# The first image's chain: one activation table load, weights quantized later, the ring cleared by GpSimd, two PSUM banks for one convolution

## The chip, the cores and the metric

The kernel runs on one core of one Trainium2 chip. The metric is the device time of a whole run in microseconds (us); smaller is better. A core has five engines with a queue of instructions each: PE (TensorE, matmuls, with PEld for its weight loads), DVE (VectorE), ACT (ScalarE), POOL (GpSimd) and SP (SyncE, which only issues DMAs here). Each engine runs its own instructions in order and waits at semaphores for the others. Sixteen DMA engines serve the core.

## The reference

The input x is 32 images of 256 channels by 32 x 32 pixels. Two layers follow each other, each with a residual:

```
x = x + conv_quant(groupnorm(x))      # 3x3, 256 -> 256 channels
x = x + involution(groupnorm(x))      # 7x7 filters made from the pixels themselves
```

`groupnorm` has 32 groups of 8 channels, without scale and shift: subtract the group's mean, divide by the root of its variance plus 1e-5. `conv_quant` rounds its input and its weights to fp16 (clipped at 65504), multiplies with fp32 accumulation, rounds and clips the result to fp16 and adds a bias. The involution makes, per pixel, 16 filters of 49 taps by two 1x1 convolutions with a fixed normalization and a ReLU between them, and applies each filter to the 16 channels of its group:

```
y   = relu(bn(w1 @ xn))                        # 64 channels
w   = w2 @ y + b2                              # 16 groups x 49 taps per pixel
out[g, c, h, w] = sum over taps of w[g, tap, h, w] * xn[g, c, neighbour(tap)]
```

## The kernel before

An image is held as a tile of 128 partitions by 2 halves of channels (`CH`) by 1024 pixels (`N`). Images go through a software pipeline that `tc.manual_schedule()` writes out by hand: the loop at L537 counts a step `n`, and in each step it asks which piece of which image is due. The order in which instructions are issued in that loop is the order in which each engine's queue holds them. An image takes `per` = 2M = 16 steps, and starts `-FRONT` = 56 steps ahead of its own sums, so that the work of about four images stands in flight.

The generator `front(b)` (L275) yields step by step the first part of image `b`'s work. In its order:

- group norm of layer 0. `add_up` (L207) sums x on ACT, one instruction per half, with the sum going into a column of `sums_sb`. `group` (L214) turns these into sums by group on DVE: transpose (L220, `across`), reduce (L222, `total`), transpose back (L226, `back`). `means` (L229) puts the mean on ACT, `squares` adds up the squares on ACT (L210 again), `variances` calls `group` again and takes the square root on ACT (L241, `s`), then `scales` and `finish` make `rstd` and `off` by eight small instructions, and `apply` writes the normalized image as fp16 into `xq` (L269, ACT).
- the convolution of layer 0. An image has four units (`units`, two halves of the pixels by two halves of the output channels). A unit is 18 matmuls from `xq` and `wq` (L320, PE) into one PSUM bank, `pc`. Then DVE clips it to fp16 (L334, `q`), adds bias and x (L336, `x`), and ACT adds up the new x for the next group norm (L210). `pc` comes from the pool `ps_c`, which has one buffer: the next unit waits for the `q` of the last.
- group norm of layer 1, then the product with `w1` (L368, `py`) and the transposes of the pixels (L383, `pt`); `py` and `pt` share one bank of the pool `ps_m` (tag "m").

After `front`, `weights` (L390) multiplies by `w2` and DVE adds `b2` while it writes the filters into a ring in SBUF, `w_sb` (L416); `scatter` (L454) sends them by DMA into the DRAM buffer `wd`, issued by SP (L465); `load_bands` (L467) reads them back as diagonals of a band matrix, issued by POOL and one in eight by SP (L478); `sums` (L489) multiplies bands and pixels on PE (L503), and `add_windows` adds them to x (L519).

Ahead of the loop stands the set-up (L122 to L194). It loads the first image, clears tiles on GpSimd, clears the ring `w_sb` on DVE (L147), loads the fp32 weights of the convolution into the first two of the three band tiles, which aren't in use yet (L154), clips and rounds them to `wq` on DVE (L155), clears the two band tiles on GpSimd (L156), and loads the small constants.

The tiles of the pool `const` lie one behind the other in SBUF in the order in which they are made, and the other pools behind them.

Of the kernel before, what the change touches and what calls it, by code (L numbers as in the profile page):

```python
# [9 lines left out]
F32 = mybir.dt.float32  # L10
AF = mybir.ActivationFunctionType
ALU = mybir.AluOpType

P = 128
B, C, H, W = 32, 256, 32, 32
N = H * W
NT = 512
RT = NT // W
CH = C // P
# [10 lines left out]
F16_MAX = 65504.0  # L30
# [35 lines left out]
FRONT = -56  # L66
# [5 lines left out]
def tile_quant_conv_then_involution(  # L72
# [16 lines left out]
    nc = tc.nc  # L89
    PSUM = bass.MemoryType.PSUM  # L90

    const = ctx.enter_context(tc.tile_pool(name="const", bufs=1))
# [7 lines left out]
    ps_m = ctx.enter_context(tc.tile_pool(name="ps_m", bufs=1, space=PSUM))  # L100
# [26 lines left out]
    xq = const.tile([P, CH, H, W], F16, name="xq")  # L127
    eps = const.tile([P, 1], F32, name="eps")
    nc.gpsimd.memset(eps, GN_EPS)
    three_halves = const.tile([P, 1], F32, name="three_halves")  # L130
    nc.gpsimd.memset(three_halves, 1.5)

# [5 lines left out]
    bands = [const.tile([P, SIDES, WINC * WB + XR], F32, name=f"band_{i}") for i in range(NBAND)]  # L138
# [5 lines left out]


    w_sb = const.tile([P, 2, RING, G, WIN], F32, name="w_sb")
    nc.vector.memset(w_sb, 0.0)  # L147
    wd = dram.tile([H, S, WPIX], F32, name="wd")
    acc = [ps_acc.tile([P, RG, NT], F32, name=f"acc_{d}") for d in range(SIDES)]

    wq = const.tile([P, CH, K0 * K0, C], F16, name="wq")
    for kh in range(CH):
        wf = bands[kh].rearrange("p d n -> p (d n)")[:, : K0 * K0 * C].rearrange("p (k c) -> p k c", c=C)
        nc.sync.dma_start(wf, w0[kh * P : (kh + 1) * P])  # L154
        nc.vector.tensor_scalar(wq[:, kh], wf, F16_MAX, -F16_MAX, ALU.min, ALU.max)  # L155
        nc.gpsimd.memset(bands[kh], 0.0)  # L156
    w2_sb = const.tile([P, K1, SW], F32, name="w2_sb")
    for i in range(2):
        nc.sync.dma_start(w2_sb[i * CR : (i + 1) * CR], w2)
# [24 lines left out]
    for col, cols, at, n in (  # L184
        (0, S, K1 * WB, XR),
        (PAD1, PAD1, 0, PAD1 * WB),
        (W, PAD1, (K1 - PAD1) * WB, PAD1 * WB),
    ):
        to = bass.AP(
            tensor=wd.tensor,  # L190
            offset=wd.offset + col * WPIX + at,
            ap=[[ROW, H], [WPIX, cols], [1, n]],
        )
        nc.sync.dma_start(to, bands[NBAND - 1][:H, 0, :n].unsqueeze(1).to_broadcast([H, cols, n]))  # L194

    class GroupNorm:

# [77 lines left out]
    def front(b):  # L275
# [30 lines left out]
        for s in range(4 * len(units) + 2):  # L306
            u, i = divmod(s, 4)
            if u < len(units):
                nt, mh = units[u]
                if i == 0:  # L310
                    pc = ps_c.tile([P, NT], F32, tag="pc", name="pc")
                for n in range(sum(CONV[:i]), sum(CONV[: i + 1])):


                    k = n if n < K0 * K0 else CH * K0 * K0 - 1 - n
                    kh, k = n // (K0 * K0), (k + K0 * K0 // 2) % (K0 * K0)
                    di, dj = k // K0 - PAD0, k % K0 - PAD0
                    r0, r1 = max(nt * RT, -di), min((nt + 1) * RT, H - di)
                    c0, c1 = max(0, -dj), min(W, W - dj)
                    nc.tensor.matmul(  # L320
                        pc.rearrange("p (r c) -> p r c", c=W)[:, r0 - nt * RT : r1 - nt * RT, c0:c1],
                        wq[:, kh, k, mh * P : (mh + 1) * P],
                        xq[:, kh, r0 + di : r1 + di, c0 + dj : c1 + dj],
                        start=n == 0,
                        stop=n == CH * K0 * K0 - 1,
                    )

            u, i = divmod(s - 3, 4)
            if 0 <= u < len(units) and i < 3:
                nt, mh = units[u]  # L330
                cols = slice(nt * NT, (nt + 1) * NT)
                if i == 0:
                    q = work.tile([P, NT], F16, tag="q", name="q", bufs=1)
                    nc.vector.tensor_scalar(q, pc, F16_MAX, -F16_MAX, ALU.min, ALU.max)  # L334
                elif i == 1:
                    nc.vector.scalar_tensor_tensor(  # L336
                        xt[:, mh, cols], q, bias_sb[:, mh : mh + 1], xt[:, mh, cols], ALU.add, ALU.add
                    )
                else:
                    gn.add_up(xt, nt, mh, nt * NT, (nt + 1) * NT, AF.Identity)  # L340
            yield
# [112 lines left out]
    def scatter(b, k):  # L454

        at = (b * H + k * TR) % RING
        for dj in range(K1):
            t, e = divmod(dj, 2)
            to = bass.AP(
                tensor=wd.tensor,  # L460
                offset=wd.offset + k * TR * ROW + dj * WPIX + (K1 - 1 - dj) * WB,
                ap=[[WPIX, TW], [ROW, TR], [1, WB]],
            )
            rows = w_sb[t * TW : (t + 1) * TW, e, at : at + TR]
            nc.sync.dma_start(to, rows.rearrange("p s g r -> p s (g r)"))  # L465
# [23 lines left out]
    def sums(b, m):  # L489

        k, d = divmod(m, SIDES)
        j0 = 0 if d else PAD1
        band = bands[(b * K + k) % NBAND][:, d]
        px = pixels[(b * K + k) % NPIX][:, d]
        for h in range(CH):
            for v in range(2):
                for g, at, top, f, l in windows(b, m):
                    p = slice(g * KP, (g + 1) * KP)
                    of = band[p, g * XR + j0 * WB : g * XR + (j0 + WINI) * WB]
                    of = of.rearrange("p (j g r) -> p j g r", g=G, r=WIN)  # L500
                    for t in range(T):
                        a = h * T + t
                        nc.tensor.matmul(  # L503
                            at[t * TW : (t + 1) * TW, h, :, f - top : l - top],
                            px[p, a, v * GC : v * GC + TW],
                            of[:, :, 2 * a + v, f - top : l - top],
                            start=(h, v) == (0, 0),
                            stop=(h, v) == (CH - 1, 1),
                        )

    def add_windows(b, m):

        d = m % SIDES
        to = x_tiles[b].rearrange("p h (r c) -> p h r c", c=W)
        j0 = d * (JC - PAD1)
        for g, at, top, f, l in windows(b, m):
            x_at = to[:, :, f:l, j0 : j0 + WINI]
            of = at.rearrange("p h j r -> p h r j")[:, :, f - top : l - top]
            nc.vector.tensor_tensor(x_at, of, x_at, ALU.add)  # L519

    def store(b, k):

        cols = slice(k * NT, (k + 1) * NT)
        nc.sync.dma_start(out[b].rearrange("(h p) n -> p h n", p=P)[:, :, cols], x_tiles[b][:, :, cols])
# [5 lines left out]
    def due(n, lag):  # L530

        b, i = divmod(n - lag, per)
        return (b, i) if 0 <= b < B else (None, None)

    with tc.manual_schedule():
        fronts = {}
        for n in range(FRONT, B * per + 2):  # L537
            b, i = due(n, FRONT)
            if i == 0:
                fronts[b] = front(b)  # L540
            later = list(fronts)
            for part in range(2):
                for b in list(later):
                    got = next(fronts[b], fronts)
                    if got is fronts:
                        fronts.pop(b)
                    if got is not LATER:
                        later.remove(b)
            b, i = due(n, 0)
            if b is not None and i % 2 == 0:  # L550
                sums(b, i // 2)
            b, i = due(n, 1)
            if b is not None and i % 2 == 0:
                add_windows(b, i // 2)
                if i // 2 == M - 1:
                    store(b, 1)
                    x_tiles.pop(b)

            b, i = due(n, 2)
            if b is not None and i == 2 * (M - 1 - SIDES):  # L560
                store(b, 0)
            b, i = due(n, -LEAD)
            if b is not None and i % 2 == 0:
                weights(b, i // 2 * WR)

            b, i = due(n, -LEAD + 1)
            if b is not None and i % 2 == 0:
                for k in range(K):
                    if i // 2 == min((k + 1) * TR // WR, H // WR - 1):
                        scatter(b, k)  # L570
            b, i = due(n, LOAD)
            if i == 0 and b > 0:
                x_tiles[b] = load_x(b)

            b, i = due(n, 3 - 4 * NBAND)
            if b is not None and i % 4 == 0:
                load_bands(b, i // 4)
# [37 lines left out]
```

## Time and profile before

| | us |
|---|---|
| median of 3 runs | 1411.43 (1402.78, 1411.43, 1411.64) |
| the profiled execution's own time | 1416.45 |
| its span, first to last instruction | 1414.7 |

| engine | busy us | share of the span | instructions |
|---|---|---|---|
| PE | 1265.2 | 89% | 29440 |
| DVE | 933.0 | 66% | 3180 |
| ACT | 729.8 | 52% | 1699 |
| POOL | 1003.5 | 71% | 1817 |

The row of the page that shows the DMA engines' busy share in 40 slices of the span, 35.4 us each, begins with 6, 0 and 9: busy while the first inputs are loaded, then idle, then busy at nine tenths to the end. By queue, q1 (issued by SP) carried 235.72 MB in 279904 packets and took 57.2% of the 16 engines' time; q0 (issued by POOL) carried 129.14 MB and took 34.5%.

A line of the timeline has the start and the duration in us, the engine, the line of the kernel, the operation, the output and input with their shapes, and the number of merged instructions. In brackets stands the idle time of the engine just before it, and what ended that idle time.

### The profile page before, as it was taken

To read this page: it belongs to the slowest core of one execution; us is meant where nothing else is said; L and a number is where in the kernel's file an instruction comes from. 1 tells how busy PE (TensorE), PEld (TensorE's weight loads), DVE (VectorE), ACT (ScalarE), POOL (GpSimd) and SP (SyncE) were. 2 spreads that over 40 slices of the span, in tenths; PEclk is the share of its full clock that TensorE was granted. 3 is DMA by queue.
4 is the path that set the end of the run, shared out by engine and by line. 5 is a ranking of instruction groups with operands and counts; after the bars stand their busy time and mean duration, and the time that the engine had idled before them with its cause. 6 is when DMAs were issued, how large, how long until landed. Compare 5 with 4: busy or idle time off the path is not lost.

```text
span 1414.7 us, 70076 instructions
## 1 busy us (share of the span) xinstructions
PE 1265.2 (89%) x29440; PEld 802.2 (57%) x29440; DVE 933.0 (66%) x3180; ACT 729.8 (52%) x1699; POOL 1003.5 (71%) x1817
## 2 busy tenths in 40 slices
PE   4899899999999899989999999999999999999665
PEld 1456565566565566655566556565566556655543
DVE  4567667767677677766767667767667676766642
ACT  5775555455555445555545555554556454553300
POOL 7067767686776777767777777677776767777774
PEclk9999999999999999999999999999999999999976
DMA  6099899999999999999999999999999999999995
GB/s 212 6 228 283 251 277 276 281 262 285 277 273 264 287 268 269 294 260 270 289 267 287 268 277 253 273 280 273 274 289 271 268 279 282 278 270 262 258 258 165
DMA packets 366232, 369.33 MB, mean 261 GB/s; under 512 B 78624, under 2 KB 308192, under 8 KB 365664
## 3 DMA queue, kind: packets, MB, share of 16 engines
q1 hardware_dynamic: 279904, 235.72, 57.2%
q0 software_dynamic: 86016, 129.14, 34.5%
q8 instruction: 234, 3.83, 1.2%
q14 instruction: 78, 0.64, 0.1%
HBM read 183.81 MB, written 180.74 MB: 258 GB/s over the span
## 4 chain that ended last, share of the span: by engine, by line
PE 47%; DMA 31%; issue 7%; POOL 5%; DVE 4%; ACT 3%; SPq 2%; POOLq 0%; DVEq 0%; ACTq 0%
DMA band<-wd 24%; PE pc L320 19%; PE acc L503 15%; PE pw L398 9%; DMA wd<-w_sb 7%; POOL band L478 5%; PE py L368 3%; DVE w_sb L416 2%; PE pt L383 2%; SPq L465 2%; ACT junk L210 1%; DVE x L519 0%; DVE w_sb L147 0%; ACT xn L269 0%; DVE q L334 0%
## 5 line engine op out<-in xcount | busy, mean ns | idle before, releaser
L478 POOL DMA_DIRECT2D band<-wd x1792 | 978.0, 548 | 397.8 <-DMA band<-wd 249.0
L416 DVE TENSOR_TENSOR w_sb<-pw,b_sb 128x16 f32<-128x16 f32 (+9 forms) x1920 | 454.0, 350 | 386.9 <-PE pw L398 363.2
L320 PE MATMUL pc<-xq,wq 128*128 128x496 f16 (+3 forms) x2304 | 536.5, 379 | 31.3 <-ACT xq L269 21.4
L503 PE MATMUL acc<-band,pixels 64*32 64x190 f32 (+1 forms) x16384 | 420.5, 323 | 78.9 <-DMA band<-wd 39.6
L503 PEld LDWEIGHTS acc<-band,pixels 64*32 64x32 f32 x16384 | 298.3, 108 | 171.1 <-issue 101.5
L320 PEld LDWEIGHTS <-wq 128*128 128x128 f16 x2304 | 206.4, 98 | 328.9 <-issue 114.6
L398 PE MATMUL pw<-w_sb,y 64*32 64x224 f32 (+1 forms) x8192 | 296.6, 333 | 31.1 <-issue 29.4
L519 DVE TENSOR_TENSOR x<-acc,x 128x380 f32<-128x380 f32 (+1 forms) x512 | 261.7, 511 | 35.7 <-PE acc L503 26.8
L398 PEld LDWEIGHTS pw<-w_sb,y 64*32 64x32 f32 x8192 | 182.8, 107 | 63.0 <-issue 43.9
L387 ACT COPY pixels<-pt 128x512 f32<-128x512 f32 x128 | 73.6, 575 | 238.2 <-PE pt L383 238.2
L210 ACT ACTIVATE junk<-x 128x512 f16<-128x512 f32 (+1 forms) x192 | 146.5, 763 | 20.7 <-DVE x L336 15.2
L210 ACT ACTIVATE junk<-x,mean 128x1024 f16<-128x1024 f32 x128 | 147.1, 1149 | 4.3
L241 ACT ACTIVATE s<-back,eps 128x2 f32<-128x2 f32 x64 | 18.9, 296 | 193.7 <-DVE back L226 193.6
L334 DVE TENSOR_SCALAR q<-pc 128x512 f16<-128x512 f32 x128 | 87.2, 682 | 16.5 <-PE pc L320 16.3
L269 ACT ACTIVATE xn<-x,off,rstd 128x512 f32<-128x512 f32 x128 | 96.1, 799 | 0.0
L336 DVE SCALAR_TENSOR_TENSOR x<-q,bias_sb,x 128x512 f32<-128x512 f16 x128 | 92.1, 719 | 0.2
L383 PEld LDWEIGHTS pt<-ident,xn 128*128 128x128 f32 x512 | 64.0, 142 | 27.4 <-issue 3.2
L383 PE MATMUL pt<-ident,xn 128*128 128x128 f32 x512 | 78.1, 275 | 0.9 <-ACT pixels L387 0.9
L231 ACT ACTIVATE mean<-back 128x2 f32<-128x2 f32 x64 | 12.7, 199 | 127.6 <-DVE back L226 127.6
L269 ACT ACTIVATE xq<-x,off,rstd 128x1024 f16<-128x1024 f32 x64 | 75.8, 1227 | 0.1
L368 PEld LDWEIGHTS py<-xn,w_sb 128*64 128x64 f32 x2048 | 63.0, 139 | 16.5 <-issue 8.1
L368 PE MATMUL py<-xn,w_sb 128*64 128x64 f32 x2048 | 67.8, 224 | 2.3 <-ACT xn L269 1.8
(40 smaller groups left out, 370.7 us busy)
## 6 DMA issues: line engine op xcount, KB each, us to landing
wd<-w_sb SPq DMA_DIRECT2D x896, 160.0 KB
band<-wd POOLq DMA_DIRECT2D x1792, 70.2 KB
x<-in_x SPq DMA_DIRECT2D x64, 512.0 KB
out<-x SPq DMA_DIRECT2D x64, 512.0 KB
band<-wd SPq DMA_DIRECT2D x256, 70.2 KB
band<-in_w SPq DMA_DIRECT2D x2, 1152.0 KB
w_sb<-in_w SPq DMA_DIRECT2D x2, 196.0 KB
wd<-band SPq DMA_DIRECT2D x2, 180.0 KB
```

What stands on the lines that cost most here:

```text
L210: nc.scalar.activation(junk[:, n0:n1], src[:, h, n0:n1], func, bias=bias, accum_out=self.sums[:, i : i + 1])
L269: nc.scalar.activation(dst, src, AF.Identity, bias=self.off[:, one], scale=self.rstd[:, one])
L320: nc.tensor.matmul(pc.rearrange("p (r c) -> p r c", c=W)[:, r0 - nt * RT : r1 - nt * RT, c0:c1], wq[:, kh, k, mh * P : (mh + 1) * P], xq[: ...
L334: nc.vector.tensor_scalar(q, pc, F16_MAX, -F16_MAX, ALU.min, ALU.max)
L336: nc.vector.scalar_tensor_tensor(xt[:, mh, cols], q, bias_sb[:, mh : mh + 1], xt[:, mh, cols], ALU.add, ALU.add)
L368: nc.tensor.matmul(py[i * CR : (i + 1) * CR, cols], w1_sb[:, kh, :], px[:, r : r + 2], start=kh == 0, stop=kh == CH - 1,)
L383: nc.tensor.transpose(pt[:, i, h * P : (h + 1) * P], xn[:, h, (m + i) * P : (m + i + 1) * P], ident)
L398: nc.tensor.matmul(pws[i][t * TW : (t + 1) * TW, r, : dj.stop - dj.start], y_sb[b % 2][half, (r0 // 2 + r) * W : (r0 // 2 + r + 1) * W], w ...
L416: nc.vector.tensor_tensor(to, pws[i][:p, r : r + rows, e, d0 * G : d1 * G].rearrange("p r (d g) -> p r d g", g=G), b2_sb[:p, e, d0 * G : d ...
L478: queue.dma_start(band[j::JC, :, j * WB : j * WB + WPIX], src)
L503: nc.tensor.matmul(at[t * TW : (t + 1) * TW, h, :, f - top : l - top], px[p, a, v * GC : v * GC + TW], of[:, :, 2 * a + v, f - top : l - top],
L519: nc.vector.tensor_tensor(x_at, of, x_at, ALU.add)
```

## The change

Four edits, all in the set-up or for the first image alone:

- Right behind `eps`, a one-column activation with the square root is issued on ACT, into a new tile `warm` of 128 x 1.
- The ring `w_sb` is no longer cleared on DVE in the set-up.
- The weights are only loaded in the set-up. Rounding them to `wq` and clearing the two band tiles goes into a function `quantize_weights`, which the loop calls in its third step (`n == FRONT + CH`), after the parts of `front` due in that step; the same function then clears `w_sb`, on GpSimd.
- The first image's units 1 and 3 take their PSUM bank from `ps_m` instead of `ps_c`.

```diff
     nc.gpsimd.memset(eps, GN_EPS)
+
+    warm = const.tile([P, 1], F32, name="warm")
+    nc.scalar.activation(warm, eps, AF.Sqrt)
     three_halves = const.tile([P, 1], F32, name="three_halves")
...
     w_sb = const.tile([P, 2, RING, G, WIN], F32, name="w_sb")
-    nc.vector.memset(w_sb, 0.0)
...
+    staged = []
     for kh in range(CH):
         wf = bands[kh].rearrange("p d n -> p (d n)")[:, : K0 * K0 * C].rearrange("p (k c) -> p k c", c=C)
         nc.sync.dma_start(wf, w0[kh * P : (kh + 1) * P])
-        nc.vector.tensor_scalar(wq[:, kh], wf, F16_MAX, -F16_MAX, ALU.min, ALU.max)
-        nc.gpsimd.memset(bands[kh], 0.0)
+        staged.append(wf)
...
+    def quantize_weights():
+
+        for kh in range(CH):
+            nc.vector.tensor_scalar(wq[:, kh], staged[kh], F16_MAX, -F16_MAX, ALU.min, ALU.max)
+            nc.gpsimd.memset(bands[kh], 0.0)
+        nc.gpsimd.memset(w_sb, 0.0)
...
                 nt, mh = units[u]
-                if i == 0:
+                if i == 0 and b == 0 and u % 2:
+
+                    pc = ps_m.tile([P, NT], F32, tag="m", name="pc")
+                elif i == 0:
                     pc = ps_c.tile([P, NT], F32, tag="pc", name="pc")
...
+            if n == FRONT + CH:
+                quantize_weights()
             b, i = due(n, 0)
```

In the built program, DVE's queue then begins with the three instructions of the first `group`, the two quantizations, and the next `group`; ACT's begins with the one table load and the activation into `warm`; the second table load is gone; PE, POOL and SP hold the same instructions in the same order as before, but for the memset of `w_sb` behind those of the two band tiles on POOL.

## The prediction

> **What bounds the kernel now.** I read the stage table first, because the change touches only the work of the first image and of the set-up. The columns are the stretch, its length, busy us (and instructions) of PE, PEld, DVE, ACT and POOL, then clock, DMA share and GB/s.
>
> ```profile
> 0.00:69.00 69.00, 43.11 (x325) 20.13 (x326) 32.16 (x73) 45.76 (x103) 25.46 (x25) 1.00 0.34 110
> 93.00:1350.00 1257.00, 1162.70 (x27817) 744.16 (x27818) 860.39 (x2962) 664.83 (x1550) 924.47 (x1694) 0.99 0.97 273
> ```
>
> From 93 us on the DMA engines are 97% busy and PE 92%: the long part is limited by both, and no edit speeds up either there. Before 69 us the DMA share is 0.34, nearly all of it loads. The first scatter of filters into the buffer wd is issued at 69.03 us; nothing of the long part can start without it. So the first 69 us are a prologue, and a microsecond off its chain is one off the end, unless a resource bound to absolute time takes its place. The timeline of the prologue shows that chain (start, duration, engine, line, operation; in brackets the idle time before it and who ended it):
>
> ```profile
> 4.68 1.28 ACT L210 ACT_TABLE_LOAD   x1 [4.68 <-DMA x<-in_x]
> 2.41 6.46 DVE L147 MEMSET w_sb<- 128x7680 f32 x1 [2.41 <-issue]
> 8.79 0.15 DVE L220 STREAM_TRANSPOSE across<-sums 128x32 f32<-128x32 f32 x1
> 9.08 1.88 DVE L155 TENSOR_SCALAR wq<-band 128x2304 f16<-128x2304 f32 x1
> 10.88 0.19 DVE L226 STREAM_TRANSPOSE back<-total 128x32 f32<-128x32 f32 x1
> 12.00 1.53 DVE L155 TENSOR_SCALAR wq<-band 128x2304 f16<-128x2304 f32 x1 [0.93 <-DMA band<-in_w]
> 13.93 1.28 ACT L241 ACT_TABLE_LOAD   x1
> 14.02 0.21 DVE L220 STREAM_TRANSPOSE across<-sums 128x32 f32<-128x32 f32 x1 [0.49 <-ACT junk L210]
> 15.22 0.29 ACT L241 ACTIVATE s<-back,eps 128x2 f32<-128x2 f32 x1
> 26.28 3.97 PE L320 MATMUL pc<-xq,wq 128*128 128x512 f16 x18 [0.78 <-DVE q L334]
> 36.44 0.21 DVE L220 STREAM_TRANSPOSE across<-sums 128x32 f32<-128x32 f32 x1
> 41.53 3.97 PE L320 MATMUL pc<-xq,wq 128*128 128x512 f16 x18 [1.77 <-ACT xq L269]
> ```
>
> The reader is to see four delays: a table load after x has landed; a memset and a quantization on DVE that hold the first mean; a second table load that ends at 15.21, just ahead of s; and 0.78 us in which PE waits for DVE to empty the one bank. Against these stands one line that the change cannot move: the second half of the weights lands at 12.00.
>
> [...]L140's took 5.97 us beside the DVE memset, L156's 5.97 each without one. [...]the first 18 matmuls took 6.36 us, the next 3.97.
>
> **The change part by part**, as times of the changed kernel.
>
> *Table load.* Two loads become one. The new one waits for no DMA, so it ends before x lands at 4.68; the warm activation needs eps, set at 0.98. The first sum starts at 4.7 instead of 5.98, the second when the other half of x is there (not later than 7.16; I take 5.9), and both end at 7.1, at worst 8.3.
>
> *DVE memset and order.* The memset moves to GpSimd, the quantizations behind the first mean's three instructions. The group step takes 0.7 us (from 14.02 to 14.7 in its second use), so the mean is at 7.8 instead of 11.10, and the squares end at 10.6 (2.5 us plus 0.3 for the mean). That alone would be 3.3 us. But in the new order of DVE both quantizations now stand ahead of the variance's transpose. The second waits for its DMA until 12.00 and takes 1.53: the transpose starts at 13.55 instead of 14.02, a gain of 0.47. The other 2.9 us are lost to this wait, and with them the worry over when x lands: up to 2.9 us later costs nothing. With 1.88 us, the first quantization's time, the gain would be 0.1.
>
> *Second table load gone.* s then follows at 13.55 + 0.7 = 14.25 instead of 15.22: **0.97 us** in all (0.6 to 1.0). PE starts at 18.17 instead of 19.14.[...]
>
> *Two banks.* Unit 0 ends at 24.54, and units 1, 2, 3 follow without the three waits of 0.78: at 24.55, 28.52, 32.49, ending at 36.46 (before: 39.76). Units 2 and 3 need q of units 0 and 1, done at 25.3 and 29.2. But PE is not what comes next: the second image's convolution waits for its xq on ACT (1.77 us in the last line above). That chain goes over DVE, where image 1's variance transpose stands behind x of unit 2. x of unit 2 comes 0.97 + 2 x 0.78 = 2.53 us earlier, at 33.2; the squares end at about 33.6, so the transpose stays bound by DVE and starts at 33.9 instead of 36.44. xq starts 3.8 us after it as before, at 37.7, and PE at 39.0 instead of 41.53. xq has one buffer and must wait for unit 3 to have read it, 36.46: slack 1.2 us. So **2.53 us** in all; the third 0.78 goes into PE's idle time. What is late next is ACT's chain.
>
> *GpSimd.* Its order gets one memset more, behind the two of the bands (to 26.0, as they still start at 14.14 behind the pixels' memsets). At L156's rate, 5.97 us for 7048 elements, 7680 take 6.5: done at 32.5. The first instruction that waits for it writes the ring at 60.81 - 2.5 = 58.3, and GpSimd's next own work, the band loads, stood at 77.32: cover of 26 and 42 us. No DMA issue moves past another on SP's or POOL's queue. What is new is that x of units 0 and 1[...] run beside a GpSimd memset. If they doubled to 1.5 us, unit 0's has 0.7 us of slack before unit 1's x, and unit 1's has about 0.35 before the squares bind: at most 0.4 us lost, below nothing excluded. I take 0.
>
> *One small tile more.* warm takes 32 bytes, and in the built program every tile behind it moves up by 32 (w_sb from 129312 to 129344). Taken as 0; see the last rival.
>
> Sum: -2.53 us.[...] Against the profiled execution's own 1416.45 us (span 1414.7 and 1.75 around it) that is 1413.9. The median shown is 5.0 us lower, at 1411.43; the forecast is set against it: **1408.9 us**. The three runs lie 9 us apart, more than three times the gain.
>
> **The rivals.**
>
> *Only the start counts.* If the second image's chain on ACT is held by something else (for example its x landing later than it now needs it), the banks bring nothing: -0.97, 1410.5. For it: image 1's x was issued at only 21.65. Against it: its first sum started at 27.91 with no wait for a DMA, and ACT wants it at about 26.9.
>
> *The gain is absorbed.* From 93 us on, PE and DMA take turns at the end of waits, and an earlier start may be spent in a different interleaving: 1411.4. Against it: between 40 and 70 us the DMA queues carry almost nothing (a share of 0.01), so the limiting stream itself starts earlier.
>
> *Slower: the shifted addresses.* [...]The 896 scatters of 160 KB are 229,376 rows. [...]queue 1 spent 57.2% of 16 x 1414.7 us on 279,904 packets, 46 ns each[...].
>
> **How the numbers follow.** Within 1% (14 us, about what can be told from no change) lies nearly everything above. The forecast's case gets 0.72, with a range of its own from 1401 to 1413 by the spread of the runs; only the start 0.06, absorbed 0.10, addresses 0.08 (of which 0.03 above 1%), unseen causes 0.04 on either side. Range: the runs' spread of 1402.8 to 1411.6 less 2.5 below[...]: **1400 to 1416**. Chances: faster 0.04, same 0.91, slower 0.05.
>
> **What would show it.** One table load, done before 4.7; the first mean near 7.8; the variance's transpose right behind a quantization that starts at 12.00; s near 14.25; no gap between the first image's four units; image 1's convolution near 39.0; the first scatter near 66.5. If that scatter comes 2.5 us early and the end doesn't, the gain was absorbed; if queue 1's share rises above 58%, the addresses cost. The forecast is wrong if the weights land at another time than 12.00, or if the long part's length between first scatter and end differs by more than the gain.

## The result and the profile after

Over 20 runs each, the median is 1405.6 us (1396.03 to 1412.58) against 1410.24 (1393.54 to 1419.45) before. The ratio of the runs is 0.9973, with a 95% interval of 0.995 to 0.9996: faster by 3.8 us, between 0.6 and 7.1. (The two medians lie 4.6 us apart.) The profiled execution took 1399.26 us, with a span of 1397.5.

The timeline of the changed kernel, with the lines that answer to those of before:

```profile
0.74 1.28 ACT L132 ACT_TABLE_LOAD   x1 [0.74 <-PEq L618]
...
6.99 0.21 DVE L229 STREAM_TRANSPOSE across<-sums 128x32 f32<-128x32 f32 x1 [6.99 <-ACT junk L219]
...
7.71 0.20 ACT L240 ACTIVATE mean<-back 128x2 f32<-128x2 f32 x1 [0.82 <-DVE back L235]
...
8.51 1.76 DVE L201 TENSOR_SCALAR wq<-band 128x2304 f16<-128x2304 f32 x1 [0.84 <-DMA band<-in_w]
...
12.08 1.44 DVE L201 TENSOR_SCALAR wq<-band 128x2304 f16<-128x2304 f32 x1 [1.81 <-DMA band<-in_w]
...
13.44 0.19 DVE L229 STREAM_TRANSPOSE across<-sums 128x32 f32<-128x32 f32 x1
...
14.14 0.30 ACT L250 ACTIVATE s<-back,eps 128x2 f32<-128x2 f32 x1 [3.62 <-DVE back L235]
...
18.06 18.05 PE L332 MATMUL pc<-xq,wq 128*128 128x512 f16 x72 [18.06 <-ACT xq L278]
...
38.81 3.97 PE L332 MATMUL pc<-xq,wq 128*128 128x512 f16 x18 [2.71 <-ACT xq L278]
...
66.34 11.95 SPq L477 DMA_DIRECT2D wd<-w_sb  x14
```

The mean is 3.4 us earlier than before (7.71 for 11.10), but s only 1.08 (14.14 for 15.22): in between, ACT is idle for 3.62 us, waiting behind the second quantization, which waits for its weights until 12.08 and ends at 13.52. The four units of the first image are now one row of 72 matmuls without a gap. Image 1's convolution starts at 38.81, after 2.71 us in which PE is idle. The first scatter is issued at 66.34 instead of 69.03; its line before was

```profile
69.03 12.12 SPq L465 DMA_DIRECT2D wd<-w_sb  x14
```

The stage table shows the long part as busy as before (length, busy us of PE, PEld, DVE, ACT and POOL, clock, DMA share, GB/s):

```profile
91.00:1333.00 1242.00, 1157.73 (x27700) 740.74 (x27683) 858.57 (x2960) 663.34 (x1548) 920.82 (x1688) 0.99 0.98 276
```

The two spans differ by 17.2 us, and only 2.69 of these lie ahead of the first scatter. The other 14.5 lie in the long part, which the change doesn't touch: 1331.2 us from first scatter to end here, 1345.7 before. The same length was between 1316 and 1346 us in the 14 profiles of this study. It shows no pattern by kernel, but one by chip: the four shortest come from the chip on which the kernel before is some 8 us faster too. So a single execution says nothing on a change of this size. The time of the first scatter says more, though it also moves between executions of one kernel, as a second profile of the change will show; the medians of many runs tell within some 3 us.

### The profile page after: what moved, and what is told of

It is laid out like the page before. It is cut to its first block, busy times and chain, and to the rows that moved or that the text cites. A ratio compares the mean times of both kernels' runs of the same rounds, so it can differ in the third digit from the quotient of the medians.

```text
span 1397.5 us, 70073 instructions
## 1 busy us (share of the span) xinstructions
PE 1263.0 (90%) x29440; PEld 801.1 (57%) x29440; DVE 926.6 (66%) x3179; ACT 727.9 (52%) x1699; POOL 1009.8 (72%) x1818
## 4 chain that ended last, share of the span: by engine, by line
PE 49%; DMA 30%; issue 6%; POOL 5%; DVE 4%; SPq 3%; ACT 2%; POOLq 0%; DVEq 0%; ACTq 0%
DMA band<-wd 23%; PE pc L332 20%; PE acc L515 15%; PE pw L410 9%; DMA wd<-w_sb 6%; POOL band L490 5%; PE py L380 3%; SPq L477 3%; DVE w_sb L428 2%; PE pt L395 2%; ACT junk L219 1%; DVE x L531 1%; DMA band<-in_w 1%; DMA x<-in_x 0%; ACT xn L278 0%
## 5 line engine op out<-in xcount | busy, mean ns | idle before, releaser
L332 PE MATMUL pc<-xq,wq 128*128 128x496 f16 (+3 forms) x2304 | 535.1, 378 | 28.1 <-ACT xq L278 21.3
```

The source lines that it names most:

```text
L332: nc.tensor.matmul(pc.rearrange("p (r c) -> p r c", c=W)[:, r0 - nt * RT : r1 - nt * RT, c0:c1], wq[:, kh, k, mh * P : (mh + 1) * P], xq[: ...
```

## The experiments

Each kernel is compared with runs of the kernel before on the same chip, in the order in which they stand here. Those medians were 1410.6 us for the first four kernels, 1411.5 for the next three, 1402.3 for the next four and 1410.8 for the last. The first scatter is read from one profile each. Six of the kernels were run once (the banks alone, the order alone, order and banks, the change once more, the memsets behind at first, the second bank for unit 1); of these only the profile is used, but for one time that is taken up at the end.

**The banks alone.**

```diff
# on the kernel before
-                if i == 0:
+                if i == 0 and b == 0 and u % 2:
+                    pc = ps_m.tile([P, NT], F32, tag="m", name="pc")
+                elif i == 0:
```

> The kernel before with the two-bank edit alone. Theory of the prediction (the banks take two of the three waits of 0.78 us off the second image's chain, through the variance's transpose that stands on DVE behind x of unit 2): xq for the first image as before (about 17.9 us), no gap between the first image's four units, image 1's convolution at about 40.0 instead of 41.5, and the first scatter at 67.4 to 67.5 instead of 69.0 (1.56 us earlier). Rival, that ACT's chain is held by something else, such as the second image's load: the gaps go, but the first scatter stays at 68.8 to 69.1.

Measured: xq at 17.87 as before, no gaps, and these two rows on PE:

```profile
19.15 16.79 PE L323 MATMUL pc<-xq,wq 128*128 128x512 f16 x72 [19.15 <-ACT xq L269]
38.65 5.66 PE L323 MATMUL pc<-xq,wq 128*128 128x512 f16 x18 [2.71 <-ACT xq L269]
```

Image 1's convolution starts at 38.65, 2.88 us earlier than before. About 1.9 of this are the two waits: from one q to the next there are 3.81 us instead of 4.75. The other 1.0 comes from a shorter cold phase, by which is meant the slow start of the first image's matmuls (before, its first 18 took 6.36 us and each later 18 took 3.97): the first q already stands at 24.54 instead of 25.54 although PE started as before. But its first 18 matmuls then took 5.66 us instead of 3.97, after PE had been idle for 2.71. The first scatter stands at 67.81 rather than 67.4: the mechanism holds for image 1's convolution, and a cost of 1.7 us shows that neither theory had.

**The order alone.** Both quantizations behind the first mean; two table loads, the ring's memset on DVE and one bank as before.

```diff
# on the kernel before
-        nc.vector.tensor_scalar(wq[:, kh], wf, F16_MAX, -F16_MAX, ALU.min, ALU.max)
-        nc.gpsimd.memset(bands[kh], 0.0)
+        staged.append(wf)
...
+            if n == FRONT + CH:
+                quantize_weights()      # without the memset of w_sb
```

> The kernel before with one edit alone: both quantizations of the weights go behind the first mean; two table loads, the ring's memset on DVE and one PSUM bank stay as they were. Theory (the landing of the second half of the weights at about 12.0 us sets the variance's transpose, so that everything ahead of it has slack): s at 14.1 to 14.3 us although the second table load is still there, since it now falls into the wait for the weights; the first scatter at about 68.0, the whole 1.0 us of the start. Rival (the table loads and the memset are worth what they take): s no earlier than 14.7, and the first scatter at 68.5 or later.

Measured: first scatter 67.88, 1.15 us earlier than before, and on ACT and DVE:

```profile
12.27 1.28 ACT L247 ACT_TABLE_LOAD   x1
...
14.14 0.29 ACT L247 ACTIVATE s<-back,eps 128x2 f32<-128x2 f32 x1 [0.59 <-DVE back L232]
```

The second table load is still there, but it is over at 13.55, and s waits for DVE all the same. s stands at 14.14, exactly where the whole change has it.

**Order and banks, without the table load and the ring edits.** The last two diffs together; against the change it reads

```diff
-    warm = const.tile([P, 1], F32, name="warm")
-    nc.scalar.activation(warm, eps, AF.Sqrt)
...
+    nc.vector.memset(w_sb, 0.0)
...
-        nc.gpsimd.memset(w_sb, 0.0)
```

> The change without its table load edit and without moving the ring's memset to GpSimd: the reordered quantizations and the two banks alone. Theory of the weights' landing: the two edits left out are worth nothing, so the first scatter stands where the whole change has it, 66.3 us, within 0.2. Rival (each edit has its share): 66.8 or later.

Measured: first scatter 66.22, against 66.34 in the whole change. The first mean comes 1.7 us later than there (9.44), and s at 14.14 all the same. Two of its four edits, the warm activation and the ring's move to GpSimd, bring nothing beside the other two.

**The addresses alone.**

```diff
# on the kernel before
     nc.gpsimd.memset(eps, GN_EPS)
+    pad = const.tile([P, 1], F32, name="pad")
+    nc.gpsimd.memset(pad, 0.0)
```

> The kernel before with one more 128 x 1 tile behind eps, cleared by GpSimd and never read, so that all tiles behind it move up by 32 bytes as in the change; nothing else. Theory: addresses cost nothing, ratio 1.000 within its interval (0.998 to 1.002), share of queue 1 57.0 to 57.6%, 46 ns a packet. [...]Second rival (the shift helps and is the part of the gain above 2.5 us): ratio about 0.999.

Measured: ratio 1.001 (0.9986 to 1.0033), queue 1's share 57.4%. No cost of the shift is seen; one of more than 4.7 us lies outside the interval.

**The second quantization later.**

```diff
# on the change
             if n == FRONT + CH:
-                quantize_weights()
+                quantize_weights(0)
+            if n == FRONT + 6:
+                quantize_weights(1)     # and the memset of w_sb
```

> The change with the second quantization moved once more, behind the variance's group step and the reciprocal, so that only PE's second nine matmuls need it. Theory (the wait for the second half of the weights costs 2.9 us): the variance's transpose follows the squares at about 10.6 us, s at 11.3 instead of 14.1, PE's first matmul at about 15.2 instead of 18.1. What is late next is the second image's x, issued at 21.35 us and landed at about 28: so its squares and what follows come only 0.5 to 1.5 us earlier, and the first scatter stands at 64.9 to 65.9 instead of 66.3. Rival (x of image 1 lands early enough): first scatter at 63.5. Other rival (the wait was hidden): 66.3.

Measured: s at 13.61, first scatter 68.17, ratio 0.9979 (0.9962 to 0.9997). The expectation failed, and for a reason outside all three theories. DVE and POOL, with the rows that matter:

```profile
8.57 4.42 DVE L200 TENSOR_SCALAR wq<-band 128x2304 f16<-128x2304 f32 x1 [0.81 <-DMA band<-in_w]
...
14.02 6.22 DVE L200 TENSOR_SCALAR wq<-band 128x2304 f16<-128x2304 f32 x1
```

```profile
7.65 4.13 POOL L146 MEMSET pixels<- 128x768 f32 x6
13.05 5.97 POOL L201 MEMSET band<- 128x7048 f32 x1 [1.27 <-DVE wq L200]
20.30 5.97 POOL L201 MEMSET band<- 128x7048 f32 x1 [1.27 <-DVE wq L200]
```

Both quantizations end 1.2 us after a memset: the first at 12.99, after the last of the pixels' memsets had ended at 11.78, and the second at 20.24, after the band's memset that was running when it started had ended at 19.02. In the change the pixels' six memsets took 6.55 us, and 6.55 - 4.13 = 2 x 1.21. So here the two kinds of instruction shut each other out. Each quantization ended only behind a memset that ran beside it; whether one gets in ahead of the next memset is open. Image 1's first sum over the second half waited for its DMA until 28.21, as expected of its x; and its first unit took 5.65 us, after 3.37 us of idle PE.

**Image 1's x earlier as well.**

```diff
# on the last kernel
+    x_tiles[1] = load_x(1)
     bn = const.tile([P, 4], F32, name="bn")
...
-            if i == 0 and b > 0:
+            if i == 0 and b > 1:
                 x_tiles[b] = load_x(b)
```

> As the run before, with the second image's x loaded ahead of the small constants of the normalization, about 7 us earlier. Theory: no wait is left for it, so the whole 2.85 us of the start go through: PE's first matmul at 15.2, image 1's convolution at about 36.0, first scatter at 63.4 to 63.7. Time against the kernel before: 5.5 us less, ratio 0.996. Rival (x of image 1 was no limit): the same first scatter as the run before.

Measured: here the quantizations got in (1.70 and 1.69 us; the first began at 8.58, where the one kept out in the last kernel began at 8.57), the transpose followed the squares at 10.71, s at 11.42, PE's first matmul at 15.34, image 1's convolution at 35.94, all as expected. So the wait for the weights did cost 2.7 us. But PE had been idle for 3.13 us, its next 18 matmuls took 5.65, and the first scatter stands at 65.13 instead of 63.45. Ratio 0.9961 (0.9943 to 0.9978).

**A delay on purpose.** 26 more activations of image 0's x on ACT, into the scratch tile `junk`, ahead of its first sum.

```diff
# on the change
         gn.begin(1)
+        for _ in range(26 if b == 0 else 0):
+            junk = work.tile([P, N], F16, tag="junk", name="junk", bufs=1)
+            nc.scalar.activation(junk, xt[:, 0], AF.Identity)
```

> The change with 26 more activations over the first half of image 0's x on ACT ahead of its first sum, into the scratch tile, about 1.1 us each: the first scatter comes about 28 us later than in the change, at about 94. Theory (the prologue goes through to the end one for one): the time rises by the same 28 us over the change and by about 25 over the kernel before, ratio 1.018 (1.015 to 1.021). Rival (the long part takes up part of an earlier or later start): a rise of at most half of it, ratio below 1.009.

Measured: first scatter 92.79, 23.8 us later than before; time 1430.12, ratio 1.0151 (1.0109 to 1.0194), so 21.3 us more (15 to 27). The mean moved by 28.4 us, but s by only 25.6: with the weights there long before, the 2.8 us of waiting for them fell away. Taken against the scatter, 0.90 of a delay reaches the end (0.65 to 1.15). The rival's half at most is excluded; one for one is not.

**The change once more**, the same file.

> The change itself once more. In its profile PE stood idle for 2.71 us ahead of image 1's convolution and then ran at full speed (18 matmuls in 3.97 us); in other kernels of this study an idle time of 2.70 to 3.37 us was followed by 5.65 us. Theory (the same idle time is or isn't followed by slow matmuls from one execution to the next[...]): the first unit of image 1 takes either 3.97 or about 5.65 us, and the first scatter stands at 66.3 or 68.0, give or take 0.9 for the first image's cold phase. Rival (the kernels differ, not the executions): 3.97 and 66.3 again.

Measured: first scatter at 74.22.

```profile
9.57 1.39 DVE L201 TENSOR_SCALAR wq<-band 128x2304 f16<-128x2304 f32 x1 [1.98 <-DMA band<-in_w]
...
12.94 5.97 POOL L202 MEMSET band<- 128x7048 f32 x1
...
13.85 6.28 DVE L201 TENSOR_SCALAR wq<-band 128x2304 f16<-128x2304 f32 x1 [2.89 <-DMA band<-in_w]
...
20.04 0.19 DVE L229 STREAM_TRANSPOSE across<-sums 128x32 f32<-128x32 f32 x1
...
20.74 0.30 ACT L250 ACTIVATE s<-back,eps 128x2 f32<-128x2 f32 x1 [10.31 <-DVE back L235]
```

The weights landed 1.8 us later. That alone would have moved s by 1.8. But by then the first band's memset had begun, 0.9 us earlier, and it held the quantization until 18.91. s comes 6.6 us later than in the other profile of the same kernel. Then PE idled for 2.71 us again, and this time its matmuls were slow: the stage table for the first and the second unit of image 1 (clock third from the right) reads

```profile
45.03:50.70 5.67, 5.65 (x18) 2.19 (x18) 0.77 (x4) 4.38 (x8) 0.00 (x0) 0.70 0.01 3
51.47:55.45 3.98, 3.97 (x18) 1.76 (x18) 1.42 (x5) 2.49 (x11) 0.00 (x0) 1.00 0.00 0
```

so the granted clock was 0.70 of full speed on average in the one and 1.00 in the other. Both delays come and go between executions of one kernel. The 0.9 us allowed for the cold phase was the author's estimate; in the ten profiles with the first image's 72 matmuls in one row, these took 16.79 to 18.11 us.

What goes with the slow matmuls stands in the clock's record. It begins, at full speed, where the first image's matmuls turn fast: at 29.30 us here, at 23.46 in the other profile of the change, and at 24.02 in that of the kernel before, where one matmul began 0.37 to 0.43 us after the last up to 23.7 us and 0.20 to 0.22 from 24.05 on. In these two other traces the clock is either 1.00 or 0.50, and from one change to the next it lasted 3.413 us or a whole multiple of it (the first two stretches of before: 136.53 and 3.41 us). Cut into such steps, the stretch ahead of image 1 reads here

```profile
42.95:46.36 3.41, 1.32 (x7) 0.63 (x7) 0.86 (x2) 3.35 (x7) 0.00 (x0) 1.00 0.01 2
46.36:49.77 3.41, 3.41 (x10) 1.27 (x9) 0.77 (x4) 2.40 (x6) 0.00 (x0) 0.50 0.02 5
```

and in the other profile

```profile
33.70:37.11 3.41, 2.40 (x12) 0.98 (x11) 1.73 (x7) 2.55 (x11) 0.00 (x0) 1.00 0.00 0
37.11:40.53 3.42, 1.72 (x9) 0.81 (x9) 0.51 (x1) 3.36 (x7) 0.00 (x0) 1.00 0.01 2
```

Here 2.09 of the 2.71 idle us lie in one step, and the next step runs at half speed. There a boundary cuts the same idle time into 1.01 and 1.70, and the clock stays.

**GpSimd's memsets behind the quantizations.**

```diff
# on the change
-    for t in pixels:
-        nc.gpsimd.memset(t, 0.0)
...
             nc.vector.tensor_scalar(wq[:, kh], staged[kh], F16_MAX, -F16_MAX, ALU.min, ALU.max)
-            nc.gpsimd.memset(bands[kh], 0.0)
-        nc.gpsimd.memset(w_sb, 0.0)
+        for t in bands[1::-1] + pixels + [w_sb]:
+            nc.gpsimd.memset(t, 0.0)
```

> The change with GpSimd's memsets of the pixels and of the two band tiles put behind both quantizations, so that nothing runs on GpSimd beside them. Theory (the quantization, a one-input instruction from SBUF to SBUF, and a memset on GpSimd shut each other out; alone it takes 1.2 us, and the rest of its 1.4 to 1.9 us, or of the 4.4 and 6.2 us in the run with the late second quantization, is waiting): both quantizations take 1.15 to 1.25 us, the variance's transpose starts at about 13.3, and the pixels' memsets take 0.69 us each instead of 1.09. Rival (the instruction itself takes 1.4 to 1.9 us, and the 4.4 and 6.2 were another accident): 1.4 or more.

Measured, with GpSimd idle beside DVE:

```profile
8.51 1.36 DVE L199 TENSOR_SCALAR wq<-band 128x2304 f16<-128x2304 f32 x1 [0.80 <-DMA band<-in_w]
11.79 1.36 DVE L199 TENSOR_SCALAR wq<-band 128x2304 f16<-128x2304 f32 x1 [1.92 <-DMA band<-in_w]
13.06 0.20 DVE L227 STREAM_TRANSPOSE across<-sums 128x32 f32<-128x32 f32 x1
```

```profile
25.03 4.14 POOL L201 MEMSET pixels<- 128x768 f32 x6
```

The memsets take 0.69 us each, as expected. The quantization takes 1.36 us by its record, not the expected 1.2, and its last 0.09 overlap what follows on DVE; of the 1.4 to 2.0 us beside the pixels' memsets, at most 0.6 are waiting. First scatter 65.62. The time of this one run, 1383.8 us, is taken up again below.

**The second bank for unit 1 alone.**

```diff
# on the change
-                if i == 0 and b == 0 and u % 2:
+                if i == 0 and b == 0 and u == 1:
```

> The change with the second bank for unit 1 alone, units 0, 2 and 3 in the first. Theory (the third of the three waits of 0.78 us goes into PE's idle time): PE waits 0.78 us ahead of unit 3 and is idle for 1.93 instead of 2.71 us ahead of image 1; image 1's convolution starts at 38.8 as in the change, give or take 0.9 for the first image's cold phase, and its first unit takes 3.97 us. Rival (the third wait is on the path): image 1's convolution 0.78 later, at 39.6.

Measured:

```profile
32.66 3.97 PE L332 MATMUL pc<-xq,wq 128*128 128x512 f16 x18 [0.78 <-DVE q L346]
38.39 3.97 PE L332 MATMUL pc<-xq,wq 128*128 128x512 f16 x18 [1.76 <-ACT xq L278]
```

Image 1 starts no later (38.39; 38.81 in the change), with the third wait of 0.78 us back in place. The 0.4 us between the two are the cold phase: the first three units take 13.81 us here and 14.24 in the change. That wait is worth nothing on the path, and with it PE's idle time is 1.76 us; none of the five idle times of 0.97 to 1.77 us in this study was followed by slow matmuls. First scatter 65.92.

**The best of it together.** The kernel with the late second quantization and the early x, the memsets behind, and a filling:

```diff
# on the kernel with the early x, with the memsets moved as in the run with them behind
+            if b == 0 and s == 15:
+                fill = ps_c.tile([P, NT], F32, tag="pc", name="fill")
+                for n in range(10):
+                    nc.tensor.matmul(fill, wq[:, 0, 0, :P], wq[:, 0, 0:2], start=n == 0, stop=n == 9)
```

> The late second quantization and the early load of image 1's x, with GpSimd's memsets behind the quantizations and ten matmuls of weights by weights in the free bank behind the first image's last unit, whose result nobody reads. Theory: nothing shuts out the quantizations, PE stays fast into image 1 (3.97 us for its first unit), and the first scatter stands at 63.4 (0.9 either way for the cold phase), against 65.1 without the filling matmuls and 66.3 in the change. Time 5.6 us below the kernel before, ratio 0.996 (0.9935 to 0.9985). Rival (the idle time is not what makes those matmuls slow): the first unit of image 1 takes 5.65 us again.

Measured:

```profile
33.13 2.32 PE L342 MATMUL fill<-wq 128*128 128x512 f16 x10
36.42 3.97 PE L331 MATMUL pc<-xq,wq 128*128 128x512 f16 x18 [0.97 <-ACT xq L277]
```

s at 11.46, image 1's first unit at full speed, first scatter 63.95, 5.1 us before that of the kernel before. Time 1393.84 (1391.1 to 1398.6, 10 runs), ratio 0.9936 (0.9907 to 0.9965): 9 us less, between 5 and 13. It is faster than the kernel before, and its ratio is below that of the change (0.9973), though the intervals of the two meet. The prologue explains only the near end of its interval. Without the filling, an estimate by the steps of 3.413 us from where this profile's matmuls turn fast (20.51), 2.3 us of idle PE would lie in one step.

**The memsets behind, timed.** The single 1383.8 us asked for it.

> The kernel with GpSimd's memsets behind both quantizations once more, now timed. Its one run took 1383.8 us beside a kernel before at 1402.3, far more than the 3.4 us by which its first scatter came early. Theory (only the prologue counts): first scatter at 65.6, a cold phase or a cold restart aside, and the time 3 to 5 us below the kernel before, ratio 0.9965 to 0.998, with a smaller spread, as no quantization can be shut out for 6 us. Rival (something in the long part is faster): the ratio of that one run, about 0.987.

Measured: first scatter 66.22; 1408.22 us over 22 runs (1400.46 to 1420.09), ratio 0.9996 (0.9975 to 1.0016). The rival is excluded: the single run was far from this kernel's usual time. The expected 3 to 5 us and the smaller spread aren't seen either; of the 2.8 us that its scatter is ahead, the interval holds up to 3.5 as well as a loss of 2.3. At this size the time of the whole kernel doesn't decide.

All kernels that were timed in several rounds, with the first scatter's distance to before (69.03) beside that of the time, in us:

| kernel | first scatter | time (95% interval) |
|---|---|---|
| the change | -2.7 | -3.8 (-7.1 to -0.6) |
| address shift alone | +0.5 | +1.4 (-2.0 to +4.7) |
| late second quantization | -0.9 | -3.0 (-5.4 to -0.4) |
| and early x | -3.9 | -5.5 (-8.0 to -3.1) |
| delay | +23.8 | +21.3 (+15 to +27) |
| best | -5.1 | -9.0 (-13.0 to -4.9) |
| memsets behind | -2.8 | -0.6 (-3.5 to +2.3) |

Each interval holds its scatter's distance, the best one's only just. That scatter is from one profile each, and differs between executions: by 7.9 us in the two profiles of the change, by 0.6 in the two with the memsets behind.

## Why the prediction was right, and where it was not

**The bound and the pass-through** held. A prologue ends with the first scatter; it came at 66.34 where 66.5 was forecast. The delay showed that what is lost there is lost at the end, to within a third, so that "the gain is absorbed" falls. The time fell by 3.8 us (0.6 to 7.1) where 2.53 were forecast; the interval is too wide to tell the two apart. That the scatter moved by 2.69 is closer than the terms deserve, as the next two parts show. (The weights of the cases also come to 1.04 if the 0.04 for unseen causes is counted on either side.)

**The start** held in its sum: s at 14.14 (forecast 14.25), PE at 18.06 (18.17). The first mean came at 7.71 (7.8), and its advance went, as forecast, into the wait for the second half of the weights. The step that failed is the split of that sum: 0.47 us was put down to the order and 0.5 to "second table load gone". The order alone brought all of it, with both loads in place, since the load then falls into the wait. The two "parts" were not independent, and only the run with one of them shows it.

The two numbers of the start, a landing at 12.00 and 1.53 us for the quantization, were right in their sum alone. With the banks alone the second half landed at 11.55, 0.45 us before that:

```profile
11.55 1.97 DVE L155 TENSOR_SCALAR wq<-band 128x2304 f16<-128x2304 f32 x1 [0.49 <-DMA band<-in_w]
```

```profile
11.58 0.73 POOL L143 MEMSET pixels<- 128x768 f32 x1
12.26 1.94 POOL L143 MEMSET pixels<- 128x768 f32 x1
```

The quantization ended at 13.52 all the same, 1.21 us after the memset that ended at 12.31. So it was in all seven profiles in which the weights landed beside these memsets: landing from 11.55 to 12.08, end from 13.52 to 13.56. The end was set by GpSimd's memsets, which the change leaves where they were, and part of the 1.53 us was waiting. With the memsets behind, a landing at 11.79 put s at 13.77. The forecast took both numbers from one profile, in which they fit together, and its sum came true for a reason it didn't have. Its sign "the forecast is wrong if the weights land at another time than 12.00" fails the same way: with the second bank for unit 1 alone they landed at 11.69 and s stood at 14.14, while a landing at 13.85 cost 6.6 us.

**The banks** held: two of the three waits counted, and the third did not, as the run with the second bank for unit 1 alone confirms. Each wait was worth more than the 0.78 that was put down for it, because a unit in an unbroken row takes less than the 3.97 us of a unit by itself:

```profile
28.52 0.69 DVE L346 TENSOR_SCALAR q<-pc 128x512 f16<-128x512 f32 x1 [1.11 <-PE pc L332]
...
32.33 0.69 DVE L346 TENSOR_SCALAR q<-pc 128x512 f16<-128x512 f32 x1 [1.75 <-PE pc L332]
```

From q to q these are 3.81 us, for 4.75 before (3.97 and 0.78): 0.94 a wait, 1.88 for two instead of 1.56. Against that the cold phase took 0.25 us more than before, so that unit 0's q came 0.83 earlier and not 1.08. 0.83 and 1.88 make the 2.7 us by which image 1's convolution moved, where the forecast had 0.97 and 1.56. The two misses nearly cancel.

The sentence that the third wait "goes into PE's idle time" took that idle time for harmless. It grew from 1.77 to 2.71 us, and in the 14 profiles an idle time of 2.70 to 3.37 us ahead of image 1 was followed by 18 matmuls in 5.65 us rather than 3.97 in five of nine cases; one of 0.97 to 1.77 in none of five. The prediction counted a cold phase for the first image only. What differed between the two groups was how the steps of 3.413 us cut the idle time: in the five profiles with slow matmuls, the largest part of it in one step was 2.09, 2.33, 2.52, 2.71 and 2.71 us; in the other four it was 1.70, 1.80, 1.81 and 2.06. The first step began 5.40 us after PE's first matmul in the change's first profile and 4.65 us after it in the second, so the fast first unit of image 1 in the first was luck.

**GpSimd** was taken as free cover. For the ring's memset it is: done at 32.46, forecast 32.5, long before its first reader, and x of units 0 and 1 took 0.75 us beside memsets, so the 0.4 us allowed for them were not lost. The quantizations, though, were given 1.53 to 1.88 us, and their own neighbours on GpSimd were not priced: 4.4 and 6.3 us in two profiles. The forecast looked for a delay beside GpSimd in x of units 0 and 1 and not in the quantizations. Of the memsets of before it gave a time only for those of the bands, 5.97 us each with and without a memset on DVE; but two of the pixels' six took 1.94 us there, the others 0.73, and the two quantizations beside them 1.88 and 1.53 instead of the 1.36 with GpSimd idle. A single execution can therefore show a loss, as one of the change has its scatter 5.2 us after that of before. The kernel before has the same two instructions in the same order ahead of its variance, so it should be open to the long wait too; its one profile shows only the short ones.

**The addresses**, the rival on the other side, fell: the shift alone moved the time by -0.14 to +0.33%. The cost that its chances rested on was the author's estimate, which nothing in the traces shows.

**The rival "only the start counts"** fell with the banks: added to the order alone, with s at 14.14 in both, they moved image 1's convolution from 40.38 to 38.73 and the first scatter from 67.88 to 66.22.

## What to carry to other kernels

When work ahead of a steady stream is shortened, find the load that lands last and ask of each edit whether its gain comes before or behind that landing; in front of it, edits share one gain, and the order of one queue can be worth more than the instructions taken out (here 1.15 us at the first scatter, against none for the table load and the ring's memset). A wait removed from an engine that is not next on the path only makes its idle time longer, which can cost more than the wait: 0.78 us removed here, and 1.68 us lost on 18 matmuls (5.65 for 3.97) in the executions in which the clock fell. A gain of 0.2% is better judged by the moment at which the first transfer of the long part is issued than by the time of the whole; that moment has its own scatter, so it takes more than one profile.

## What the runs showed of the hardware that was not expected

- A quantization on DVE (128 x 2304, fp32 to fp16, SBUF to SBUF) and a memset on GpSimd did not slow each other, one waited for the other: in the second profile of the change, 6.28 us for an instruction that took 1.36 with GpSimd idle, ending 1.2 us after a memset of 5.97 that kept its usual duration. In the other direction six memsets took 4.13, 5.34 or 6.55 us, as none, one or two quantizations got in between them.
- After 2.7 us of idle PE, 18 matmuls took 5.65 us at a granted clock of 0.70 in one execution and 3.97 in another of the same kernel. Ahead of image 1, the clock was at 0.50 after the five steps of 3.413 us with 2.09 to 2.71 us of idle PE in them, and stayed at 1.00 after the four with 1.70 to 2.06. Over the whole traces of the kernel before and of the change's first profile, the 21 full-speed steps that were followed by one at 0.50 had 1.77 to 3.41 us of idle PE, and those followed by another at full speed had at most 1.94.
- A switch of activation tables cost its 1.28 us and no more: in the kernel before, the second began at 13.93 and the next activation at 15.22, 0.01 us after its end.
